# Two graph layers in fp32 on one core: the steps at the seams, the later normalisation and the last group's softmax moved

## The chip, the cores and the metric

The kernel runs on one core of a Trainium2 chip. The time is device microseconds of one execution; three executions were timed, and the median counts. The engines are called as the profile calls them: PE (TensorE, matrix products), PEld (its weight loads), DVE (VectorE), ACT (ScalarE), POOL (GpSimd) and SP (SyncE, which here only issues the DMAs).

## What is computed

The input x is 128 graphs of 64 nodes with 768 features, with one 64x64 adjacency per graph. Everything is fp32. Two layers follow each other:

```python
# layer 0: 12 heads of 64
h = einsum('bnd,ade->bane', x, W);  th = tanh(h)
attn = leaky_relu(th . w_src + (th . w_dst)^T, 0.2)
attn = softmax(where(adj, attn, -999))
feat = elu(attn @ h + b);  gate = sigmoid(x @ H_w.T + H_b)
x = layernorm(x + gate * feat + (1 - gate) * x)
# layer 1: 6 heads of 128
q, k, v = x @ Wq + bq, x @ Wk + bk, x @ Wv + bv
ctx = softmax(q @ k^T / sqrt(128) + where(adj, 0, -9e15)) @ v
x = layernorm(x + ctx @ Wf + bf)
```

## The kernel before

**Tiles and phases.** The 8192 rows (graph, node) are 64 tiles of 128 rows, two graphs each. Phase A computes layer 0 and layer 1's v. It takes the tiles in 32 pairs (NP = 32). Phase B computes the rest of layer 1 in 16 groups of four tiles (NG = 16). Between the phases x1 (the result of layer 0), its transpose and v lie in DRAM (x1_d, xT_d, v_d).

**Products by fewer blocks.** Each large product is taken by block schemes that trade matrix products for additions: in phase A, 7 block products for 8 (class Product, matmuls at L208), in phase B a scheme of 15 steps (R = 15, class Stream, L849). The sums of input blocks are made by `sums` (POOL, L257 to L260) in phase A, by `group_sum` (L819) for q and k and `pair_sum` (L831) for the output projection in phase B. The results of some block products are copied out of PSUM first (`snap`, ACT, L404; the first eviction of a q or k block, ACT, L870), the others are added to them (DVE, L427 and L446; L875 and L892).

**The order of the work** is written out by hand. Each phase has a dictionary of steps; `at(step, f)` appends a call to a step, and `run` makes the calls step after step, in a step in the order in which they were appended. This is the order of each engine's instructions; an engine takes its own in that order, and semaphores hold it where data or a buffer is missing. All DMAs are issued from SP in the same way. A step corresponds to one block product of PE.

**Phase A.** A pair p starts at o = 21p (N = 21). Its seven products with W (h, steps o to o+6) are followed by seven for the gate (G, o+7 to o+13), and seven for v of an earlier pair (V; own V at o+56 for most). Ahead of it come the turns of its input, `xT` (DVE stream transposes, L383, at o-6 and o-5), and `sums` (o-4). Its two tiles go through Tile0, tile 1 with s = o and tile 0 with s = o+5: tanh (L463), multiplications with w_dst and w_src on POOL (L467, L475), the exchange of the destination scores through DRAM (`dst_out`, `exchange`, `dst_in`), `gate_in` (POOL, L580) and `gate` (L584), `add` (POOL L515, leaky ReLU on ACT L518), `mask` and `top` (DVE L522, L526), `exp` (12 ACT instructions, L531), `scale` (DVE L539, POOL L541), `probs` (PE transposes L552), `aggregate` (PE L570), `elu`, `mix1`, `mix2`, `norm1` (DVE, then POOL L295 to L298), `norm2` (ACT, L302), `spill` (store of x1). The last pair has its x1 transposed on PE (`transposed`, L398) instead of being read back. At the start the weights come in: six rows of H_w (`load_hrow`, turned on PE by `hw_blocks`, L358 and L360), W, and the broadcast rows ws_bc, wd_bc, b_bc and hb_bc.

**Phase B.** A group has N = 90 steps: four streams q, k, q, k for the two column halves j, then `scores` and `scores_read`; two output streams F (one for each pair q of the group's tiles) run as fifth and sixth stream beside the next group's work. The softmax of a tile is sm_top (DVE), sm_sub (DVE), sm_exp (ACT, L939), sm_total (DVE), sm_scale (DVE, POOL L948); then `probs` (PE L954, ACT copy L960) and `context` (PE L974). After an output stream norm1 to norm3 normalise its two tiles, norm3 on ACT (L302), and `store` writes them. `load_x` and `add_bf` (POOL, L807) put x1 and the bias into xs ahead of the output stream. The last group's output streams come directly after its own q and k streams, and its tiles end with `end_stats` and `end_norm`.

The steps that the change touches stand in these lines:

```python
at(o - 6, lambda d=d: xT(d, 0))
at(o - 5, lambda d=d: xT(d, 1))
at(o - 4, lambda d=d: sums(d))
for i, s in ((1, o), (0, o + 5)):
    at(s + 19, lambda t=t: t.exp(0))
eng = nc.vector if g <= 1 and k % 2 else nc.gpsimd
sm = o + 4 * R + 8 if last else o + N + 5
t = f + R + 1 + 2 * i
at(t + 3, lambda d=d, q=q, i=i: norm3(d, q, i))
at(t + 5, lambda g=g, d=d, q=q, i=i: store(g, d, q, i))
```

Of the kernel before, what the change touches and what calls it, by code (L numbers as in the profile page):

```python
# [15 lines left out]
P = 128  # L16
# [45 lines left out]
def kernel(  # L62
# [242 lines left out]
    def phase_a(ctx):  # L305
# [35 lines left out]
        ws_bc = rows(k3, w_src.rearrange("a e o -> (a e o)"), "ws_bc")  # L341
        wd_bc = rows(k3, w_dst.rearrange("a e o -> (a e o)"), "wd_bc")
        b_bc = rows(k3, b, "b_bc")
# [18 lines left out]
        for oc in range(NC):  # L362
            load_hrow(oc)
        hb_bc = rows(k3, H_b, "hb_bc")
# [264 lines left out]

        def dense(d, key, i):  # L630
            d[key].matmuls(i)
            d[key].evict(i)
# [17 lines left out]
        for p in range(NP):  # L650
# [11 lines left out]
            if p:  # L662
                at(o - 20, lambda d=d: xb_in(d, 0))
                at(o - 16, lambda d=d: xb_in(d, 1))
                at(o - 6, lambda d=d: xT(d, 0))
                at(o - 5, lambda d=d: xT(d, 1))
            else:
                at(0, lambda d=d: d.update(T=[transposed(t) for t in d["x"]]))
            at(o - 4, lambda d=d: sums(d))
# [5 lines left out]
            for i, s in ((1, o), (0, o + 5)):  # L675
                t = Tile0(p, i)
                at(s + 6 + (i == 0), t.tanh, t.cap)
                at(s + 7, t.dst_mul)
                at(s + 8, t.src_mul)
                at(s + 9, t.dst_sum, t.dst_out, t.exchange)  # L680
                at(s + 10, t.src_sum)
                at(s + 13, t.dst_in)
                at(o + (14 if i else 16), t.gate_in)
                at(o + (16 if i else 18), t.gate)
                at(s + 17, t.add)
                at(s + 18, t.mask, t.top)
                at(s + 19, lambda t=t: t.exp(0))

                at(s + (19 if i else 20), lambda t=t: t.exp(1))
                at(s + 21, lambda t=t: t.scale(0))  # L690
                at(s + 22, lambda t=t: t.scale(1))
                at(s + 24, t.probs)
                at(s + 25, t.aggregate)
                at(s + 26, t.elu)
                at(s + 27, t.mix1)
                at(s + 28, t.mix2)
                at(s + 29, t.norm1)
                at(s + 30, t.norm2)
                at(s + 31, t.spill)
# [13 lines left out]
            else:  # L713
                for i in range(2):
                    at(o + 42 + i, lambda d=d, i=i: x1T(d, i, transposed(d["x"][i])))
# [12 lines left out]
            if p != NP - 4:  # L728
                at(o + (47 if p < NP - 1 else 44), lambda d=d: x1_sums(d))

            v = o + {NP - 4: 84, NP - 2: 50, NP - 1: 45}.get(p, 56)
# [25 lines left out]
        at(o + 30, lambda: load_T4(0))  # L757
        run(events, N * NP + 60)
# [3 lines left out]
    def phase_b(ctx, wq, wk):  # L762
# [167 lines left out]
        def sm_top(d, q, i):  # L930
            d["mx", q, i] = small.tile([P, HEADS], F32, name="mx1")
            nc.vector.tensor_reduce(d["mx", q, i], sm_part(d, q, i), AX.X, ALU.max)
# [103 lines left out]
        for g in range(NG):  # L1036
# [7 lines left out]
            for k in range(len(SUMS)):  # L1044

                eng = nc.vector if g <= 1 and k % 2 else nc.gpsimd
# [13 lines left out]
            for j in range(2):  # L1060
# [7 lines left out]
                for nb in range(3):  # L1068
                    at(b0 + 1 + 2 * nb, lambda d=d, j=j, nb=nb: scores_read(d, j, nb))

            sm = o + 4 * R + 8 if last else o + N + 5
            for q in range(2):
                f = o + ((6 if last else 10) + q) * R
                for i in range(2):
                    t = sm + 4 * (2 * q + i)
# [5 lines left out]
                    at(t + 2, lambda g=g, q=q, i=i: load_v(g, q, i))  # L1081
# [3 lines left out]
                pr = sm + 8 * q + 8  # L1085
# [19 lines left out]
                for i in range(2):  # L1105
# [3 lines left out]
                    at(t + 3, lambda d=d, q=q, i=i: norm3(d, q, i))  # L1109
                    at(t + 5, lambda g=g, d=d, q=q, i=i: store(g, d, q, i))  # L1110
            if g == 0:
                load_adj(0)
# [41 lines left out]
```

## Time and profile before

| | |
|---|---|
| median of 3 runs | 2963.09 us (2961.6 to 2963.64) |
| profiled execution | 2965.06 us |
| its span | 2962.8 us |
| granted PE clock, mean | 0.99 |
| PE busy | 2853.1 us, 18108 instructions |
| DVE busy | 1805.7 us |
| POOL busy | 1649.2 us |
| ACT busy | 1060.1 us |
| DMA, of 16 engines | 33.9% |

The span is the time from the profile's first to its last instruction; the time of the execution holds a little more. A group of the page reads: line, engine, operation, what is written and read (partitions x elements, type), how many; then busy time in all, mean ns of one; then the idle time of the engine just before them and what ended most of it. A row of waits names who waited, for whom, and gives the microseconds in all, how often, and the longest. In the timeline a row begins with start and duration, and the bracket at its end holds the idle time before it and what ended it. A row of windows gives the stretch, its length, and the busy time (instructions) of PE, PEld, DVE, ACT and POOL, then the granted PE clock, the DMA share and GB/s.

### The profile page before, as it was taken

How to read it: one execution, taken by the hardware profiler on the slowest of the kernel's cores; microseconds unless marked ns; L12 is line 12 of the kernel's file. 1: busy time of each engine (PE TensorE's matmuls, PEld its weight loads, DVE VectorE, ACT ScalarE, POOL GpSimd, SP SyncE). 2: the span in 40 equal slices, each digit the busy share in tenths (PEclk: the TensorE clock that was granted, in tenths of full speed). 3: DMA queues.
4: the chain of work that ended last, by engine and by line, in shares of the span. 5: the costliest groups of instructions: out<-in, count | busy, mean ns of one | idle time of the engine just before them, and what ended most of it. 6: DMA issues, size and time to landing. Idle time of an engine off the chain costs nothing.

```text
span 2962.8 us, 50018 instructions
## 1 busy us (share of the span) xinstructions
PE 2853.1 (96%) x18108; PEld 2064.4 (70%) x18108; DVE 1805.7 (61%) x3715; ACT 1060.1 (36%) x2967; POOL 1649.2 (56%) x1712
## 2 busy tenths in 40 slices
PE   7899999999999999999889999999999999999997
PEld 4455555555555555555558888888888888888886
DVE  4667767767667667677565555555555555555556
ACT  3454554554554545545522211222211222221121
POOL 3766566666666665665673454345454345545345
PEclk9999999999999999999999999999999999999999
DMA  6254454453453444544540211212211212221221
GB/s 183 84 148 127 129 148 121 132 149 112 133 149 114 139 136 120 147 125 131 158 161 18 86 59 60 87 55 87 87 66 59 81 56 85 86 70 60 76 81 70
DMA packets 358965, 309.13 MB, mean 104 GB/s; under 512 B 226624, under 2 KB 304192, under 8 KB 358720
## 3 DMA queue, kind: packets, MB, share of 16 engines
q1 hardware_dynamic: 358720, 305.95, 33.6%
q8 instruction: 144, 2.36, 0.3%
q14 instruction: 101, 0.83, 0.1%
HBM read 192.19 MB, written 101.06 MB: 99 GB/s over the span
## 4 chain that ended last, share of the span: by engine, by line
PE 45%; POOL 23%; DVE 15%; ACT 9%; issue 4%; DMA 3%; SPq 1%; POOLq 0%; DVEq 0%
PE X L849 30%; PE X L208 9%; ACT s L531 6%; POOL S L819 5%; POOL gt L580 4%; POOL Sc L831 3%; DVE s L522 2%; DMA xT_d<-T 2%; DVE nmx L526 2%; POOL xs L807 2%; POOL th L475 2%; PE pb L974 2%; POOL s L541 2%; PE pb L914 2%; POOL rstd L295 2%
## 5 line engine op out<-in xcount | busy, mean ns | idle before, releaser
L208 PE MATMUL X<-w,S 128*128 128x384 f32 x2304 | 800.7, 493 | 29.5 <-ACT snap L404 28.0
L849 PE MATMUL X<-S,w 128*128 128x256 f32 x2816 | 668.1, 382 | 20.7 <-ACT q L870 15.9
L208 PEld LDWEIGHTS X<-w,S 128*128 128x128 f32 x2304 | 429.9, 191 | 326.1 <-issue 42.4
L208 PE MATMUL X<-w,T 128*128 128x384 f32 x1728 | 603.6, 492 | 14.7 <-DVE T L383 12.6
L849 PEld LDWEIGHTS X<-S,w 128*128 128x128 f32 x2816 | 522.7, 190 | 99.1 <-issue 21.2
L208 PEld LDWEIGHTS X<-w,T 128*128 128x128 f32 x1728 | 329.7, 193 | 240.3 <-issue 25.1
L831 POOL TENSOR_TENSOR Sc<-cT 128x256 f32<-128x256 f32 x224 | 161.0, 728 | 381.2 <-PE X L849 377.6
L849 PE MATMUL X<-w,Sc 128*128 128x256 f32 x1408 | 328.2, 385 | 3.9 <-DVE xs L892 2.7
L892 DVE TENSOR_TENSOR xs<-xs,X 128x256 f32<-128x256 f32 x512 | 208.6, 419 | 180.0 <-PE X L849 148.7
L849 PEld LDWEIGHTS X<-w,Sc 128*128 128x128 f32 x1408 | 264.9, 191 | 47.0 <-DVE xs L892 9.8
L531 ACT ACTIVATE s<-s,nmx 128x64 f32<-128x64 f32 x768 | 256.1, 335 | 94.6 <-DVE nmx L526 94.6
L875 DVE TENSOR_TENSOR k<-k,X 128x256 f32<-128x256 f32 x320 | 133.5, 421 | 218.6 <-PE X L849 168.4
L875 DVE TENSOR_TENSOR q<-q,X 128x256 f32<-128x256 f32 x320 | 132.0, 419 | 204.7 <-PE X L849 121.0
L541 POOL TENSOR_TENSOR s<-s,rs 128x384 f32<-128x384 f32 x128 | 128.7, 1005 | 214.2 <-DVE rs L539 145.6
L849 PE MATMUL X<-xb,w 128*128 128x256 f32 x960 | 236.6, 379 | 0.0
L302 ACT ACTIVATE xs<-xs,shift,rstd 128x768 f32<-128x768 f32 x62 | 63.7, 1027 | 473.7 <-POOL shift L298 464.7
L404 ACT COPY snap<-X 128x384 f32<-128x384 f32 x288 | 136.0, 473 | 234.2 <-PE X L208 234.2
L467 POOL TENSOR_TENSOR tmp<-th,wd_bc 128x768 f32<-128x768 f32 x64 | 138.2, 2160 | 133.7 <-ACT th L463 133.7
L870 ACT ACTIVATE k<-X,bk_c 128x256 f32<-128x256 f32 x192 | 90.9, 474 | 305.2 <-PE X L849 305.2
L849 PEld LDWEIGHTS X<-xb,w 128*128 128x128 f32 x960 | 181.2, 190 | 24.0
L948 POOL TENSOR_TENSOR s<-s,rs 128x384 f32<-128x384 f32 x64 | 53.0, 828 | 242.1 <-DVE rs L947 219.3
L870 ACT ACTIVATE q<-X,bq_c 128x256 f32<-128x256 f32 x192 | 88.8, 470 | 258.6 <-PE X L849 258.6
(106 smaller groups left out, 4102.6 us busy)
## 6 DMA issues: line engine op xcount, KB each, us to landing
xb<-in_x_dram SPq DMA_DIRECT2D x64, 384.0 KB
s<-dst_d SPq DMA_DIRECT2D x128, 192.0 KB
x_d<-xb SPq DMA_DIRECT2D x64, 384.0 KB
xT_d<-T SPq DMA_DIRECT2D x64, 384.0 KB
v_d<-v SPq DMA_DIRECT2D x128, 192.0 KB
xb<-xT_d SPq DMA_DIRECT2D x32, 768.0 KB
xb<-v_d SPq DMA_DIRECT2D x256, 96.0 KB
xs<-x_d SPq DMA_DIRECT2D x64, 384.0 KB
```

What stands on the lines that cost most here:

```text
L208: nc.tensor.matmul(o, self.lhsT(i, c), rhs, start=first and c == 0, stop=last and c == CH - 1, skip_group_check=True,)
L404: nc.scalar.copy(t, ps)
L467: nc.gpsimd.tensor_tensor(self.tmp, self.th, wd_bc, ALU.mult)
L531: nc.scalar.activation(self.s[:, a], self.s[:, a], AF.Exp, bias=self.nmx[:, a : a + 1], accum_out=self.sm[:, a : a + 1],)
L541: nc.gpsimd.tensor_tensor(t, t, rs[:, :, None].to_broadcast([P, A // 2, S]), ALU.mult)
L580: nc.gpsimd.tensor_tensor(self.g, self.g, hb_bc, ALU.add)
L819: eng.tensor_tensor(t, group_part(d, r0), group_part(d, r1), op)
L831: nc.gpsimd.tensor_tensor(t, pair_part(d, q, r0), pair_part(d, q, r1), op)
L849: nc.tensor.matmul(ps, self.lhsT(r, slot, c), self.rhs(r, slot, c), start=start and c == 0, stop=stop and c == 1, skip_group_check=True,)
L870: nc.scalar.activation(o[:, b], ps, AF.Identity, bias=bias[:, hd : hd + 1], scale=1.0 if positive else -1.0)
L875: nc.vector.tensor_tensor(o[:, b], o[:, b], ps, ALU.add if positive else ALU.subtract)
L892: nc.vector.tensor_tensor(o, o, ps, ALU.add if positive else ALU.subtract)
```

## The change

Six things are changed; no product, sum or DMA of phase A is added or removed.

- The loads of the broadcast rows wd_bc, ws_bc and b_bc are issued after the six H_w rows instead of before.
- `xT` and `sums` of pairs 1, 2 and 31 come 7, 5 and 4 steps earlier (`lead`).
- In pairs 0 and 1, everything of a tile from `exp` to `spill` comes two steps later (`slow`), and tile 1's exps are appended at the very end of their step (`late`).
- In the last pair tile 0 has s = o+3, its x1T transposes come at o+41 and o+40 with tile 1 first, its x1 sums at o+42, its V at o+43.
- In phase B norm3 comes at t+4+2i and the store at t+6+2i. In group 0 the q and k sums whose number divided by 3 leaves 2 are made by POOL and the others by DVE, and `load_adj(0)`, with the fill that it makes, comes at step 16.
- The last group's softmax starts two steps earlier. Its maximum is negated, and `sm_top_exp` makes six exps with the maximum as bias and the sum as a second output; `sm_sub` and `sm_total` are left out there. `probs` comes at t+7 and `context` at t+10, the second pair of tiles 13 steps after the first. The second half's `scores_read` come in successive steps.

```diff
@@ -338,9 +338,6 @@
             )
-        ws_bc = rows(k3, w_src.rearrange("a e o -> (a e o)"), "ws_bc")
-        wd_bc = rows(k3, w_dst.rearrange("a e o -> (a e o)"), "wd_bc")
-        b_bc = rows(k3, b, "b_bc")
         w1 = weight_tile(1)
@@ -361,6 +358,9 @@
             load_hrow(oc)
+        wd_bc = rows(k3, w_dst.rearrange("a e o -> (a e o)"), "wd_bc")
+        ws_bc = rows(k3, w_src.rearrange("a e o -> (a e o)"), "ws_bc")
+        b_bc = rows(k3, b, "b_bc")
         hb_bc = rows(k3, H_b, "hb_bc")
@@ -627,6 +627,8 @@
+        late = {}
         def dense(d, key, i):
@@ -662,17 +664,23 @@
                 at(o - 16, lambda d=d: xb_in(d, 1))
-                at(o - 6, lambda d=d: xT(d, 0))
-                at(o - 5, lambda d=d: xT(d, 1))
+                lead = {1: 7, 2: 5, NP - 1: 4}.get(p, 0)
+                at(o - 6 - lead, lambda d=d: xT(d, 0))
+                at(o - 5 - lead, lambda d=d: xT(d, 1))
+                at(o - 4 - lead, lambda d=d: sums(d))
             else:
                 at(0, lambda d=d: d.update(T=[transposed(t) for t in d["x"]]))
-            at(o - 4, lambda d=d: sums(d))
+                at(0, lambda d=d: sums(d))
             at(o, lambda d=d: start_h(d))
...
                 at(o + 7 + i, lambda d=d, i=i: dense(d, "G", i))
-            for i, s in ((1, o), (0, o + 5)):
...
+            slow = 2 if p < 2 else 0
+            for i, s in ((1, o), (0, o + (5 if p < NP - 1 else 3))):
                 t = Tile0(p, i)
@@ -684,19 +692,23 @@
                 at(s + 18, t.mask, t.top)
-                at(s + 19, lambda t=t: t.exp(0))
-
-                at(s + (19 if i else 20), lambda t=t: t.exp(1))
-                at(s + 21, lambda t=t: t.scale(0))
-                at(s + 22, lambda t=t: t.scale(1))
-                at(s + 24, t.probs)
-                at(s + 25, t.aggregate)
-                at(s + 26, t.elu)
-                at(s + 27, t.mix1)
-                at(s + 28, t.mix2)
-                at(s + 29, t.norm1)
-                at(s + 30, t.norm2)
-                at(s + 31, t.spill)
+                z = s + slow
+                if slow and i:
+                    late.setdefault(z + 19, []).extend((lambda t=t: t.exp(0), lambda t=t: t.exp(1)))
+                else:
+                    at(z + 19, lambda t=t: t.exp(0))
+                    at(z + (19 if i else 20), lambda t=t: t.exp(1))
+                at(z + 21, lambda t=t: t.scale(0))
+                at(z + 22, lambda t=t: t.scale(1))
+                at(z + 24, t.probs)
+                at(z + 25, t.aggregate)
+                at(z + 26, t.elu)
+                at(z + 27, t.mix1)
+                at(z + 28, t.mix2)
+                at(z + 29, t.norm1)
+                at(z + 30, t.norm2)
+                at(z + 31, t.spill)
@@ -712,7 +724,7 @@
                 for i in range(2):
-                    at(o + 42 + i, lambda d=d, i=i: x1T(d, i, transposed(d["x"][i])))
+                    at(o + 41 - i, lambda d=d, i=i: x1T(d, i, transposed(d["x"][i])))
@@ -726,9 +738,9 @@
             if p != NP - 4:
-                at(o + (47 if p < NP - 1 else 44), lambda d=d: x1_sums(d))
-
-            v = o + {NP - 4: 84, NP - 2: 50, NP - 1: 45}.get(p, 56)
+                at(o + (47 if p < NP - 1 else 42), lambda d=d: x1_sums(d))
+            v = o + {NP - 4: 84, NP - 2: 50, NP - 1: 43}.get(p, 56)
             if p == NP - 4:
@@ -755,6 +767,8 @@
         at(o + 30, lambda: load_T4(0))
+        for step, fs in late.items():
+            events.setdefault(step, []).extend(fs)
         run(events, N * NP + 60)
@@ -927,9 +941,18 @@
-        def sm_top(d, q, i):
+        def sm_top(d, q, i, negate=False):
             d["mx", q, i] = small.tile([P, HEADS], F32, name="mx1")
-            nc.vector.tensor_reduce(d["mx", q, i], sm_part(d, q, i), AX.X, ALU.max)
+            nc.vector.tensor_reduce(d["mx", q, i], sm_part(d, q, i), AX.X, ALU.max, negate=negate)
+        def sm_top_exp(d, q, i):
+            s, mx, sm = sm_part(d, q, i), d["mx", q, i], small.tile([P, HEADS], F32, name="sm1")
+            for h in range(HEADS):
+                nc.scalar.activation(
+                    s[:, h], s[:, h], AF.Exp, bias=mx[:, h : h + 1], accum_out=sm[:, h : h + 1]
+                )
+            d["sm", q, i] = sm
@@ -1043,7 +1066,7 @@
-                eng = nc.vector if g <= 1 and k % 2 else nc.gpsimd
+                eng = nc.vector if (k % 3 != 2 if g == 0 else g == 1 and k % 2) else nc.gpsimd
                 if g == 0:
@@ -1066,23 +1089,31 @@
                 for nb in range(3):
-                    at(b0 + 1 + 2 * nb, lambda d=d, j=j, nb=nb: scores_read(d, j, nb))
-
-            sm = o + 4 * R + 8 if last else o + N + 5
+                    at(b0 + 1 + (1 if last and j else 2) * nb, lambda d=d, j=j, nb=nb: scores_read(d, j, nb))
+            sm = o + 4 * R + 6 if last else o + N + 5
             for q in range(2):
                 for i in range(2):
-                    t = sm + 4 * (2 * q + i)
+                    t = sm + 4 * i + (13 if last else 8) * q
+                    at(t + 2, lambda g=g, q=q, i=i: load_v(g, q, i))
+                    if last:
+                        at(t, lambda d=d, q=q, i=i: sm_top(d, q, i, True))
+                        at(t + 2, lambda d=d, q=q, i=i: sm_top_exp(d, q, i))
+                        at(t + 5, lambda d=d, q=q, i=i: sm_scale(d, q, i))
+                        at(t + 7, lambda d=d, q=q, i=i: probs(d, q, i))
+                        at(t + 10, lambda d=d, q=q, i=i: context(d, q, i))
+                        continue
                     at(t, lambda d=d, q=q, i=i: sm_top(d, q, i))
...
                     at(t + 7, lambda d=d, q=q, i=i: sm_scale(d, q, i))
-                    at(t + 2, lambda g=g, q=q, i=i: load_v(g, q, i))
                     at(t + 10, lambda d=d, q=q, i=i: probs(d, q, i))
...
-                pr = sm + 8 * q + 8
+                pr = sm + (5 + 13 * q if last else 8 + 8 * q)
                 for k in range(len(SUMS)):
@@ -1106,10 +1137,11 @@
                     at(t + 1, lambda d=d, q=q, i=i: norm2(d, q, i))
-                    at(t + 3, lambda d=d, q=q, i=i: norm3(d, q, i))
-                    at(t + 5, lambda g=g, d=d, q=q, i=i: store(g, d, q, i))
+                    at(t + 4 + 2 * i, lambda d=d, q=q, i=i: norm3(d, q, i))
+                    at(t + 6 + 2 * i, lambda g=g, d=d, q=q, i=i: store(g, d, q, i))
             if g == 0:
-                load_adj(0)
+                at(16, lambda: load_adj(0))
                 bf_bc = rows(k1, bf, "bf_bc")
```

## Prediction

> **What bounds the kernel.** I read the page's busy shares first, then TensorE's busy time stage by stage, its waits in each stage, and last the timeline around the waits that the change touches.
>
> ```profile
> PE 2853.1 (96%) x18108; PEld 2064.4 (70%) x18108; DVE 1805.7 (61%) x3715; ACT 1060.1 (36%) x2967; POOL 1649.2 (56%) x1712
> L849 PE MATMUL X<-S,w 128*128 128x256 f32 x2816 | 668.1, 382 | 20.7 <-ACT q L870 15.9
> ```
>
> TensorE sets the time; 2962.8 - 2853.1 = 109.7 us of the span is all that better order can win. The change adds no matmul and removes none, so only this idle time, and matmuls slowed after a wait, can move. By stage (window length, then PE, PE weight load, DVE, ACT, POOL busy):
>
> ```profile
> 0.00:175.00 175.00, 139.58 (x667) 84.08 (x668) 99.68 (x165) 75.20 (x232) 99.13 (x91) 0.93 0.50 141
> 1397.00:1540.00 143.00, 119.11 (x552) 71.99 (x553) 92.51 (x136) 57.39 (x166) 92.62 (x80) 0.93 0.49 153
> 1713.00:2850.00 1137.00, 1122.19 (x8403) 963.86 (x8404) 605.57 (x1612) 238.85 (x464) 551.66 (x677) 1.00 0.22 74
> 2850.00:2963.00 113.00, 97.47 (x779) 82.13 (x777) 62.65 (x169) 16.49 (x28) 55.48 (x76) 0.94 0.19 63
> ```
>
> Idle: 35.4 at the start, 23.9 at the seam between the phases, 14.8 in thirteen steady groups of phase B, 15.5 at the end (8.1 of it after the last matmul). The change leaves the other 20 us alone. TensorE's waits in the steady groups are a single row, and at the seams mixed ones (start, seam, end, a row or two of each):
>
> ```profile
> PE X L849 <- ACT q L870: 14.8, 13, 1.2
> ...
> PE X L208 <- ACT snap L404: 14.4, 4, 6.6
> PE X L208 <- DVE T L383: 7.0, 2, 5.6
> PE pa L358 <- DMA gt<-in_L_gnn_H_w_dram: 3.7, 1, 3.7
> ...
> PE X L208 <- DVE T L383: 5.6, 1, 5.6
> PE X L208 <- ACT snap L404: 5.0, 3, 4.0
> ...
> PE pb L954 <- POOL s L948: 3.3, 1, 3.3
> ```
>
> The steady one in the timeline:
>
> ```profile
> 1771.44 2.06 ACT L302 ACTIVATE xs<-xs,shift,rstd 128x768 f32<-128x768 f32 x2 [2.38 <-POOL shift L298]
> 1773.41 0.45 ACT L870 ACTIVATE q<-X,bq_c 128x256 f32<-128x256 f32 x1
> 1774.01 2.18 PE L849 MATMUL X<-S,w 128*128 128x256 f32 x9 [1.14 <-ACT q L870]
> ```
>
> Two normalisations of 1.03 us stand on ScalarE ahead of the q eviction that TensorE waits for.
>
> **What the Trainium skill says.** "PSUM — Partial Sum Buffer", Engine vs sequencer instructions: the queues of ScalarE, VectorE and GpSimdE are strict FIFO. The trace agrees: the q eviction above sat behind both normalisations. "TensorE: Matmul & The Clock Gate", Part 1, What's actually happening: after an idle window of about 3.4 us the clock halves until some 3.4 us of work. The trace agrees: after the 6.57 us wait at 63.93 six matmuls took 4.18 us, elsewhere 2.10. "ScalarE: Activation LUTs", Rules: about 0.3 us an ACTIVATE plus 0.83 ns an element; the trace has 0.335 us for 64 elements. "GPSIMD Engine Reference", §3: an add is 1.96 times as long as on VectorE; the trace has 1.27 us for 128x512 at L819, and the S0 share below rests on it.
>
> **Part 1, later normalisation in phase B.** norm3 goes from step t+3 to t+4 for tile 0 and t+6 for tile 1. On ScalarE the order beside each second output stream was q(step 4), norm3(0), norm3(1), q(7), exp, q(11); it becomes q(4), norm3(0), q(7), exp, norm3(1), q(11), in 14 places. norm3(0) still starts at 1771.44, when its shift is there, and ends at 1772.47. The data of q(7) came at about 1772.38, so q(7) ends at about 1772.93 instead of 1773.86, and TensorE, ready at 1772.87, resumes about 1772.98: 0.1 of the 1.14 us stays. Saved 14 x 1.03 = **14.4 us**. Behind norm3(1) stand q(11), wanted from about 1774.7, while norm3(1) ends about 1774.3 after the exp (0.51), and tile 1's store. That store goes about a microsecond later on SP's queue, in the same order there; behind it stand load_v, and load_x at 1785.64 whose data POOL first uses at 1798.87, so it is covered; uncovered, it would cost that microsecond. Bounds: 12 (0.2 us left each time) to 15.9 (all of the page's row).
>
> **Part 2, the start.** The three broadcast loads go behind the six H_w rows, two of 384 KB each to a wait: the 3.7 us gt wait goes, but the w0 sums on DVE (11th of 0.57 us operations from 16.3, so about 22.6) catch TensorE after 2.2. Pairs 1 and 2 get their turns and sums 7 and 5 steps earlier: the same 4 turns (2.45 us on DVE) and 4 POOL adds (0.99 + 1.69 + 0.99 + 0.99 = 4.66), but now in front of the previous pair's multiplies, gate and score add (L515). Tile 1's 12 exps (12 x 0.335 = 4.0 us) go behind the next pair's first snap. Pair 1: L515 starts about 56.7 instead of 54.98, then 1.47 + Prelu 0.84 + gate 0.83, so the snap ends about 60.4 against 63.78, and pair 1's W products end about 3.8 earlier. Pair 2: the 5.64 us turn wait goes, but sums stand ahead of L515 and tile 0 of pair 0 is itself two steps later; I put the snap's start about 108.3 instead of 111.69. That holds the gain at 3.4 to 3.8 in all, half speed after the snap wait staying. **-3.5**; bounds -9 (POOL's idle 2.54 and 3.71 us near 90 to 95 takes the sums in, and all three snaps come early) to +2 (none of it does, with later probs).
>
> **Part 3, the last pair.** The timeline before:
>
> ```profile
> 1407.87 0.55 POOL L295 TENSOR_TENSOR rstd<-rstd,neg_half 128x1 f32<-128x1 f32 x1 [3.71 <-DVE rstd L294]
> 1410.66 3.59 POOL L580 TENSOR_TENSOR gt<-gt,hb_bc 128x768 f32<-128x768 f32 x2
> 1414.22 1.46 POOL L515 TENSOR_TENSOR s<-s,src 128x768 f32<-128x768 f32 x1
> 1423.16 2.26 PE L208 MATMUL X<-w,S 128*128 128x384 f32 x5 [4.03 <-ACT snap L404]
> ```
>
> Pair 31's turns move ahead of pair 30's mix and batch norm on DVE (rstd +2.1), its sums (4.66) ahead of that gate and add: L515 starts at about 1422, not 1414.22. Here the exps (pair 30 isn't slow) still stand before the first snap, so W2 starts about 1429.5: late by 6.4, half speed included about 7, though the 5.63 us turn wait is gone. Given back: tile 0 two steps earlier takes the probs waits (0.92 + 2.89, and half speed, about 2.1); the x1 transposes, tile 1 first, and x1 sums and V two steps earlier take most of the 4.4 us wait. By V's last product I have +0.3. Group 0's sums on two engines (S0 0.7 on DVE against 1.3) and fill moved to step 16 take 1.1 from the q wait of 2.5. **-0.8**; bounds -8 (delay absorbed, waits gone) to +6 (delay not given back).
>
> **Part 4, the last group.** Out: four subtractions and four totals on DVE (8 x 0.55). In: 6 exps a tile with sum (6 x 0.335 = 2.0 us against 0.51) on ScalarE, busy 16.5 of 113 us. But probs come at step 73, not 78. Their scale on POOL stands behind add_bf (3.57) and the context sums, free at about 2904:
>
> ```profile
> 2899.62 3.57 POOL L807 TENSOR_TENSOR xs<-xs,bf_bc 128x768 f32<-128x768 f32 x2
> 2906.40 0.90 PE L954 MATMUL pb<-ident,s 128*128 128x128 f32 x3 [3.33 <-POOL s L948]
> ```
>
> TensorE arrives about 2898: a wait of 6.7 for 3.3 (+3.4), with slow matmuls 1.0 more; later the Sc wait (1.2), xs wait (2.3) and its half speed (1.9) go, as POOL has caught up. **-1**; bounds -6 to +3. The tail after the last matmul keeps its chain.
>
> Sum: -14.4 - 3.5 - 0.8 - 1.0 = -19.7. The profiled execution took 2965.06 (span 2962.8): 2945.4. The median is 2.0 below it: **2943**.
>
> **Rivals.** A, the seams do what the edits look like: 9 at the start, 8 at the last pair, 6 at the end, and 14.4: 2963 - 37 = 2926. For it: the named waits are there, and each edit lies before one. Against: POOL is 57 to 65% busy in these windows and the moved sums pass its queue. B, only the normalisation pays, seams cost: +6 - 14.4 = 2955; for it, the 6.4 us above. C, slower: GpSimd's queue becomes the bound at the seams, no idle absorbing what is put ahead. Price 4.66 for pair 1, 4.66 for pair 2, 9.1 for pair 31 with half speed, 6.2 at the end: 24.6 against 14.4, so 2973. It decides once more than 59% of that price isn't regained. Against: POOL's idle stretches before rstd (3.71). D, no change: norm3(1) delays q(11) as much as it did q(7), the wait only moves: 2963 - 14 + 14 = 2963 less what the seams give. Against: exp and norm3 fit before q(11) with 0.4 us to spare, which is thin.
>
> **From cases to numbers.** The forecast (2935 to 2951) 0.56, A 0.22, B 0.08, C 0.09, D 0.05. A measurement of this kernel can tell 0.2%, 5.9 us, from no change. Forecast, A and B are faster: 0.86; D same 0.05; C slower 0.09. The range leaves out C, D and the far end of A (0.06): 2926 to 2956.
>
> **What would show it.** Right: q waits in steady groups of about 0.1 us, the group from 88.3 to about 87.3; no gt wait over 1.5; the snaps of pairs 1 and 2 about 3.4 earlier; pair 31's W2 some 6 later than now against pair 30's last G, regained by its last V; a probs wait of 6 to 7 on POOL at the end. Wrong: a wait on q after step 11; longer snap waits; a last-group gap past 7 us. The least certain step is the 6.4 us of pair 31, worked by hand from queue order, and next the POOL wait at the end.

## Result and the profile after

The changed kernel takes 2965.14 us (median of four runs, 2964.37 to 2968.44), the kernel before beside it 2963.36. The ratio is 1.0007, with a 95% interval of 0.999 to 1.0025: no difference that can be told from zero. The forecast was 2943, with a range of 2926 to 2956.

The profiled span of the changed kernel is 2963.0 us, of the kernel before 2962.8. From its page, the busy times and the group of TensorE with the most idle time in front of it:

```profile
PE 2847.2 (96%) x18108; PEld 2063.0 (70%) x18108; DVE 1812.2 (61%) x3710; ACT 1063.3 (36%) x3011; POOL 1642.1 (55%) x1709
...
L208 PE MATMUL X<-w,S 128*128 128x384 f32 x2304 | 804.1, 495 | 61.5 <-ACT snap L404 55.9
```

The group stood at 29.5 us of idle time before; it is 61.5, nearly all for the snap on ScalarE. The rows of waits of TensorE at the start, at the seam between the phases (two rows) and in the last group:

```profile
PE X L208 <- ACT snap L404: 28.2, 5, 17.0
...
PE X L208 <- ACT snap L404: 22.3, 2, 18.2
PE pa L570 <- ACT pt L557: 7.3, 1, 7.3
...
PE pb L977 <- POOL s L971: 6.8, 2, 6.1
```

The snap waits were 14.4 and 5.0 us in these stretches. The wait for the probs copy (L557) is new. In the steady groups of phase B no wait of TensorE is left at all. The same stretches by busy time (length, then PE, PE weight load, DVE, ACT, POOL, granted clock, DMA share, GB/s):

```profile
0.00:175.00 175.00, 131.09 (x639) 78.17 (x640) 101.54 (x154) 69.89 (x220) 96.28 (x88) 0.90 0.50 139
...
1397.00:1540.00 143.00, 111.73 (x579) 66.90 (x578) 90.38 (x135) 55.26 (x162) 86.42 (x78) 0.90 0.43 131
...
1713.00:2850.00 1137.00, 1135.86 (x8642) 976.66 (x8635) 613.65 (x1630) 240.24 (x470) 561.78 (x690) 1.00 0.22 74
...
2850.00:2963.00 113.00, 96.19 (x778) 81.33 (x776) 58.32 (x161) 22.99 (x72) 54.78 (x76) 0.95 0.19 62
```

In the third row TensorE is busy 1135.9 of 1137 us, where it was 1122.2. In the first it has 131.1 of 175, where it had 139.6.

Busy times of fixed windows don't give a ledger, since the work slides through them. Marks do: the start of the same instruction in both traces. I took evictions on ScalarE: the last copy of an h block (L425), the copy of a gate block (L425) and the k evictions of phase B.

| mark | before | changed | difference |
|---|---|---|---|
| pair 0, last h copy | 36.58 | 33.41 | -3.2 |
| pair 3, last h copy | 172.06 | 180.29 | +8.2 |
| pair 30, gate copy | 1406.85 | 1414.82 | +8.0 |
| group 0, first k eviction | 1545.01 | 1560.00 | +15.0 |
| group 15, last k eviction | 2881.73 | 2881.55 | -0.2 |
| end of the span | 2962.8 | 2963.0 | +0.2 |

So the parts, as differences of neighbouring rows, forecast beside measured: start -3.5, measured +8.0 (to pair 30's gate copy); last pair and group 0's sums -0.8, measured +7.0; phase B -14.4, measured -15.2; last group -1.0, measured +0.4. The sum is +0.2 where -19.7 was forecast. Phase B did what was expected; two seams cost what it gained. The -3.2 in the first row is largely scatter of the first loads, as the experiments show. The profiled execution of the kernel before was 2.0 us above its median, and the medians differ by 1.8 us where the two spans differ by 0.2.

The phase B gain in the timeline, ScalarE beside a second output stream:

```profile
1785.41 1.03 ACT L302 ACTIVATE xs<-xs,shift,rstd 128x768 f32<-128x768 f32 x1 [2.38 <-POOL shift L298]
1786.34 0.45 ACT L884 ACTIVATE q<-X,bq_c 128x256 f32<-128x256 f32 x1
1786.70 0.51 ACT L962 ACTIVATE s<-s 128x384 f32<-128x384 f32 x1
1787.11 1.01 ACT L302 ACTIVATE xs<-xs,shift,rstd 128x768 f32<-128x768 f32 x1
1788.94 0.47 ACT L884 ACTIVATE q<-X,bq_c 128x256 f32<-128x256 f32 x1 [0.82 <-PE X L863]
```

The normalisation of tile 0 ends and the q eviction follows at once, as worked out; the second normalisation stands behind the exp and is done 0.8 us before the next q eviction can start, which then waits for TensorE and not the reverse.

The start, around pair 2's first snap, in the kernel before:

```profile
89.55 1.81 POOL L467 TENSOR_TENSOR tmp<-th,wd_bc 128x768 f32<-128x768 f32 x1 [2.54 <-ACT th L463]
...
96.12 1.80 POOL L475 TENSOR_TENSOR th<-th,ws_bc 128x768 f32<-128x768 f32 x1
...
103.34 1.46 POOL L515 TENSOR_TENSOR s<-s,src 128x768 f32<-128x768 f32 x1
...
111.69 0.45 ACT L404 COPY snap<-X 128x384 f32<-128x384 f32 x1
...
112.29 4.18 PE L208 MATMUL X<-w,S 128*128 128x384 f32 x6 [6.61 <-ACT snap L404]
```

And in the changed kernel:

```profile
92.88 1.85 POOL L467 TENSOR_TENSOR tmp<-th,wd_bc 128x768 f32<-128x768 f32 x1 [4.42 <-ACT th L463]
94.69 1.71 POOL L257 TENSOR_TENSOR S<-T 128x384 f32<-128x384 f32 x1
98.03 1.71 POOL L259 TENSOR_TENSOR S<-T 128x384 f32<-128x384 f32 x1
100.65 1.79 POOL L475 TENSOR_TENSOR th<-th,ws_bc 128x768 f32<-128x768 f32 x1
...
108.87 1.47 POOL L515 TENSOR_TENSOR s<-s,src 128x768 f32<-128x768 f32 x1
...
106.24 1.03 ACT L302 ACTIVATE xb<-xb,shift,rstd 128x768 f32<-128x768 f32 x1 [13.07 <-POOL shift L298]
111.86 0.46 ACT L404 COPY snap<-X 128x384 f32<-128x384 f32 x1
...
112.46 3.97 PE L208 MATMUL X<-w,S 128*128 128x384 f32 x6 [17.04 <-ACT snap L404]
```

TensorE has done pair 2's first two products and stands for 17.04 us. The wait for the turns (5.64 before) is gone, and the wait for the snap, 6.61 before, has taken it in and grown. The snap itself comes no earlier than before (111.86 beside 111.69), though pair 0's copy came 3.2 us earlier. On the way back from the snap: score add (L515) at 108.87 instead of 103.34, the multiply L475 at 100.65 instead of 96.12, and between L467 and L475 the four sums, of which three took 1.59 to 1.71 us where the same form takes 0.99 alone.

Pair 31 shows the same order:

```profile
1417.68 0.55 POOL L295 TENSOR_TENSOR rstd<-rstd,neg_half 128x1 f32<-128x1 f32 x1 [5.55 <-DVE rstd L294]
1420.48 0.99 POOL L257 TENSOR_TENSOR S<-T 128x384 f32<-128x384 f32 x1
1424.40 3.56 POOL L580 TENSOR_TENSOR gt<-gt,hb_bc 128x768 f32<-128x768 f32 x2
1427.91 1.47 POOL L515 TENSOR_TENSOR s<-s,src 128x768 f32<-128x768 f32 x1
...
1436.27 0.45 ACT L404 COPY snap<-X 128x384 f32<-128x384 f32 x1
...
1436.86 3.54 PE L208 MATMUL X<-w,S 128*128 128x384 f32 x5 [18.21 <-ACT snap L404]
```

And the new wait in the seam, at tile 0 of pair 31 (DVE, ACT, PE):

```profile
1506.30 1.90 DVE L612 SCALAR_TENSOR_TENSOR xb<-xb,pt 128x768 f32<-128x768 f32 x1
...
1508.29 0.86 ACT L557 COPY pt<-pa 128x384 f32<-128x384 f32 x2 [6.40 <-DVE xb L612]
...
1508.82 0.37 PE L570 MATMUL pa<-h,pt 64*64 64x64 f32 x1 [7.29 <-ACT pt L557]
```

The copy of tile 0's transposed probabilities waits for the last mix instruction of tile 1, since the two use one buffer of 128 x 768, and tile 0 now runs two steps earlier. Last, the probs of the last group:

```profile
2898.92 3.56 POOL L821 TENSOR_TENSOR xs<-xs,bf_bc 128x768 f32<-128x768 f32 x2
2903.12 0.83 POOL L971 TENSOR_TENSOR s<-s,rs 128x384 f32<-128x384 f32 x1
...
2904.00 0.90 PE L977 MATMUL pb<-ident,s 128*128 128x128 f32 x3 [6.06 <-POOL s L971]
```

A wait of 6.06 us on the scale that stands behind add_bf on POOL; the forecast had 6.7.

### The profile page after: what moved, and what is told of

The parts are those of the page before. It is cut to its first block, busy times and chain, and to the rows that moved or that the text cites. A ratio compares the mean times of both kernels' runs of the same rounds, so it can differ in the third digit from the quotient of the medians.

```text
span 2963.0 us, 50040 instructions
## 1 busy us (share of the span) xinstructions
PE 2847.2 (96%) x18108; PEld 2063.0 (70%) x18108; DVE 1812.2 (61%) x3710; ACT 1063.3 (36%) x3011; POOL 1642.1 (55%) x1709
## 4 chain that ended last, share of the span: by engine, by line
PE 60%; DVE 14%; POOL 10%; ACT 8%; DMA 5%; issue 3%; SPq 1%; POOLq 0%; DVEq 0%; ACTq 0%
PE X L863 42%; PE X L208 12%; ACT s L531 5%; POOL gt L580 3%; DMA xT_d<-T 2%; DVE s L522 2%; PE pb L997 2%; PE pb L928 2%; POOL s L541 2%; DVE nmx L526 1%; POOL th L475 1%; DVE pt L611 1%; DMA s<-dst_d 1%; DVE pt L602 1%; DVE pt L603 1%
## 5 line engine op out<-in xcount | busy, mean ns | idle before, releaser
L208 PE MATMUL X<-w,S 128*128 128x384 f32 x2304 | 804.1, 495 | 61.5 <-ACT snap L404 55.9
L889 DVE TENSOR_TENSOR q<-q,X 128x256 f32<-128x256 f32 x320 | 132.2, 420 | 188.6 <-PE X L863 131.1
L467 POOL TENSOR_TENSOR tmp<-th,wd_bc 128x768 f32<-128x768 f32 x64 | 136.9, 2139 | 131.5 <-ACT th L463 131.5
L833 POOL TENSOR_TENSOR S<-xb 128x512 f32<-128x512 f32 x103 | 130.7, 1282 | 84.1 <-DMA xb<-xT_d 57.2
```

The costliest lines, as they stand in the source:

```text
L208: nc.tensor.matmul(o, self.lhsT(i, c), rhs, start=first and c == 0, stop=last and c == CH - 1, skip_group_check=True,)
L467: nc.gpsimd.tensor_tensor(self.tmp, self.th, wd_bc, ALU.mult)
L833: eng.tensor_tensor(t, group_part(d, r0), group_part(d, r1), op)
L889: nc.vector.tensor_tensor(o[:, b], o[:, b], ps, ALU.add if positive else ALU.subtract)
```

## Experiments

Theory 1 was that phase B's part pays in full and that two seams give it back. For the start the question was whether the delay of pairs 0 and 1 (theory S) or the early turns and sums (rival L) cost. Where a result below has no ratio, the kernel was timed in one execution alone, so differences of two or three microseconds between such totals decide nothing. All trace comparisons below are by marks: "to pair 3" is the time from pair 0's last h copy to pair 3's, which leaves the first loads out (135.5 before; 146.9 changed); "to h" and "to k" go from pair 30's gate copy to pair 31's last h copy and to group 0's first k eviction (29.7 and 138.2 before; 35.5 and 145.2 changed). Profiles of the same code scatter. Seven kernels that are the same up to pair 3 gave 144.8 to 146.9 there. Seven with pair 31 and group 0 as changed gave 145.0 to 148.4 to k, with a mean of 146.8; the changed kernel's 145.2 is near the low end, and what a single profile tells at k is not better than about 3 us. The cause of the first scatter stands in the traces. TensorE waits 3.0 us for a snap in pair 0's V, between pair 2's gate and pair 3's h; after it come, in the changed kernel and in the run with pair 31's early turns and sums alone:

```profile
157.92 4.21 PE L208 MATMUL X<-w,T 128*128 128x384 f32 x6 [3.00 <-ACT snap L404]
161.92 3.08 PE L208 MATMUL X<-w,S 128*128 128x384 f32 x6
...
157.46 2.20 PE L208 MATMUL X<-w,T 128*128 128x384 f32 x6 [3.01 <-ACT snap L404]
159.50 2.10 PE L208 MATMUL X<-w,S 128*128 128x384 f32 x6
```

After the same wait the same twelve matmuls run slowly in one execution and at full speed in another. So matmuls can be slow after a wait that is shorter than the 3.4 us in the prediction; what decides whether they are was not tried.

**Later normalisation alone.** On the kernel before:

```diff
-                    at(t + 3, lambda d=d, q=q, i=i: norm3(d, q, i))
-                    at(t + 5, lambda g=g, d=d, q=q, i=i: store(g, d, q, i))
+                    at(t + 4 + 2 * i, lambda d=d, q=q, i=i: norm3(d, q, i))
+                    at(t + 6 + 2 * i, lambda g=g, d=d, q=q, i=i: store(g, d, q, i))
```

> The kernel before with only the later normalisation of phase B. Theory 1 (this part pays in full and the seams gave it back): no wait on the q eviction in the steady groups, and 14 to 15.5 us less than the kernel before, so about 2948.5. Rival (the later normalisation only moves the work to another wait, and the changed kernel's phase B gains for another reason): within 4 us of the kernel before.

Measured: 2947.56 us against 2962.29, ratio 0.9949 (0.9933 to 0.9966). Theory 1 holds and its rival falls. TensorE's waits in the steady groups come to 0.2 us. This kernel is faster than the kernel before and the changed kernel.

**The changed kernel without the delay.**

```diff
-            slow = 2 if p < 2 else 0
+            slow = 0
```

> The changed kernel with the delay of two steps in pairs 0 and 1, and the exps moved behind the snap, taken back; the earlier turns and sums stay. Measured at the copy of pair 3's last h block on ScalarE (172.06 before, 180.29 changed). Theory S (the delay puts the previous pair's norm chain in front of the snap on ScalarE): the 17 us snap wait goes and the copy comes at 169 to 174, the total 6 us or more below the changed kernel. Rival L (the earlier sums on POOL do it): copy at 178 or later, total within 3 us of the changed kernel.

Measured: 2962.81 us; the h copy of pair 3 at 173.90, 141.1 to pair 3. TensorE's wait for the snap at the start:

```profile
PE X L208 <- ACT snap L404: 30.9, 4, 17.4
```

A mixed answer. The copy came early enough for S, but the long wait that S blamed on the delay is still there, 17.4 us, and the total is only 2.3 us lower. So the long wait belongs to the early work, and the delay costs some 4 to 6 us elsewhere (144.8 to 146.9 to pair 3 with it, 141.1 without).

**The changed kernel without the early turns and sums of pairs 1 and 2.**

```diff
-                lead = {1: 7, 2: 5, NP - 1: 4}.get(p, 0)
+                lead = {NP - 1: 4}.get(p, 0)
```

> The changed kernel with turns and sums of pairs 1 and 2 at their old steps; the delay stays. Theory S: the copy of pair 3's last h block still comes at 176 or later, with a snap wait of 8 us or more in pair 2. Rival L: copy at 168 to 173, no snap wait over 7 us.

Measured: 2957.56 us; copy at 172.58, 139.2 to pair 3.

```profile
PE X L208 <- DVE T L383: 11.8, 2, 10.4
PE X L208 <- ACT snap L404: 8.0, 4, 3.5
```

By its letter this is rival L: the copy lies in its range and no snap wait is over 3.5 us. But to pair 3 it is still 4.8 us later than with neither part (134.4, in the next experiment), which is the delay's, and the long wait is now one for the turns, 10.4 us. Neither theory had that. Along the pairs the delay first wins: pair 1's last h copy came 36.7 after pair 0's (41.7 before), because the snap no longer stands behind 12 exps. Then it loses all of that and more: pair 2's turns stand on VectorE behind a mix that is two steps later.

**Of the start only the load order.** `slow = 0` and `lead` for pair 31 alone.

> The changed kernel with neither the delay nor the earlier turns of pairs 1 and 2; of the start only the order of the loads is changed. All theories: the gt wait at 0.6, and the copy of pair 3's last h block at about 172.06 - 3.2 = 168.9; the total 11 us below the changed kernel, about 2954. If the gain of the loads is lost again in pair 1, the copy comes at 171 or later.

Measured: 2958.80 us; 134.4 to pair 3; copy at 169.42. The seam loss of the start is gone, as all theories had it; the total is 6.3 us lower and not 11, since this profile took 148.2 to k and had a late first copy. The gain of the loads isn't there: pair 0's last h copy came at 35.01. Over all profiles of this study it came at 33.2 to 36.6 with the old order of the loads (four profiles, mean 34.3) and at 32.5 to 35.0 with the new (fourteen, mean 33.4). The wait for the first H_w rows (tile gt), 3.7 us in the profile before, was 1.8, 2.2 and 4.3 us in the three others with the old order. With the new order it was 0.6 us in the changed kernel's profile, but 2.3 to 2.4 in nine of the fourteen: on the whole it is shorter, not gone.

**Early work in pair 1, not in pair 2, no delay.**

```diff
-                lead = {1: 7, 2: 5, NP - 1: 4}.get(p, 0)
+                lead = {1: 7, NP - 1: 4}.get(p, 0)
...
-            slow = 2 if p < 2 else 0
+            slow = 0
```

> The changed kernel with the earlier turns and sums in pair 1 (and 31) but not in pair 2, and without the delay. Measured from pair 0's last h copy on ScalarE to pair 1's (41.7 before, 44.7 with both leads and no delay) and pair 3's (135.5 before, 141.1 with both leads and no delay, 134.4 with neither). Theory A (each early set of sums costs by itself, by standing ahead of the score add on POOL): 44.7 to pair 1 and 136.5 to 138.5 to pair 3. Rival (pair 2's loss follows from pair 1's): 140 or more to pair 3, or back to 135.5 if pair 1's loss is regained.

Measured: 2959.11 us; 45.1 to pair 1 and 138.5 to pair 3. Theory A holds: each early set costs by itself, pair 1's 4.1 us (138.5 against 134.4), pair 2's 2.6 more (141.1), which is little above the scatter.

**Early work as changed, the delay in pair 0 alone.**

```diff
-            slow = 2 if p < 2 else 0
+            slow = 2 if p < 1 else 0
```

> The changed kernel with the delay in pair 0 alone; leads as changed. Measured as above to pair 3's last h copy (146.9 changed). Theory A (pair 1's delay puts its norm chain ahead of pair 3's start and costs the 5 to 6 us lost there): 139 to 143, and no 3 us snap wait in pair 0's V. Rival (the loss in pair 3 follows from the lateness of POOL in pair 2): 145 or more.

Measured: 2965.72 us; 144.1 to pair 3, between the two expectations. Pair 1's delay did cost what pair 3 lost: from pair 2's gate to pair 3's h the time is 29.9 again (33.2 to 35.0 with the delay). But without it pair 2's snap is back behind the exps and waits 23.3 us, so the time to pair 3 is only 0.7 to 2.8 us shorter than with both delays, and the total is no shorter. The parts of the start are not additive one by one, and none of them pays with the leads in place.

The start as a table, to pair 3 in us:

| | no delay | delay in pair 0 | delay in pairs 0 and 1 |
|---|---|---|---|
| no early work | 134.4 | 134.1 (below) | 139.2 |
| early in pair 1 | 138.5 | | |
| early in pairs 1 and 2 | 141.1 | 144.1 | 144.8 to 146.9 |

Each row below the first is later than the first: by 4.1 and 6.7 without the delay, by 10.0 with the delay in pair 0, and by 5.6 to 7.7 with it in both. Except for the last field these are single profiles.

**The last pair as before**, in the changed kernel: `lead` without pair 31, s = o+5 for tile 0, x1T, x1 sums and V at their old steps.

> The changed kernel with pair 31 as before: neither earlier turns and sums nor tile 0, x1 transposes and V two steps earlier. Measured from pair 30's last gate copy on ScalarE to pair 31's last h copy (29.7 before, 35.5 changed) and to the first k eviction of group 0 (138.2 before, 145.2 changed). All theories: 29.7, and 137 to 138.5, since group 0's sums on two engines and the later fill stay; total about 7 us below the changed kernel. If group 0's part costs, the second stays above 140.

Measured: 2958.66 us; 30.8 to h, 138.3 to k. The seam's loss is gone. From V's last addition to the first k eviction it took 20.3 us (21.2 before): group 0's sums on two engines bring 0.9 us here, about as forecast (1.1). Over all profiles it is less: with the new sums this stretch took 20.3 us in nine and 21.9 to 22.0 in five, where in the two traces compared (changed kernel, load order alone) the same wait of 2.4 us is followed by slow matmuls in the one and not in the other. With the old sums it took 21.2 in all four. The mean gain is 0.3 us.

**Pair 31's early turns and sums alone**: as that kernel, with `lead` of 4 for pair 31.

> The changed kernel with only the earlier turns and sums of pair 31; its tile 0, x1 transposes and V are at their old steps. Theory P (the sums cost 5.8 at the h copy, and the 7.3 us wait for the one probs buffer comes from tile 0's two steps): 35.5 to the h copy, no wait over 4 us for the probs copy, and 139 to 142 to the first k eviction. Rival (the buffer wait comes from the lateness that the sums make): that wait stays at 5 or more and the k eviction at 144 or later.

Measured: 2960.69 us; 36.0 to h, 142.9 to k; no wait for the probs copy. Theory P holds in its first part: the early work costs 5.2 to 6.3 us at the h copy and still 4.6 at k (142.9, against an expected 139 to 142).

**Pair 31's tile 0, x1 and V alone**: `lead` without pair 31, the rest as changed.

> The changed kernel with pair 31's turns and sums at their old steps; tile 0, x1 transposes and V stay two steps earlier. Theory P: 29.7 to the h copy, the wait for the probs copy still 5 us or more, 140 to 144 to the first k eviction. Rival (the wait comes from the sums' lateness): no such wait over 3 us, 138 or less.

Measured: 2957.07 us; 29.7 to h, 139.2 to k, wait for the probs copy 7.3 us. That wait comes from tile 0's two steps, as P said, but it cost 1 us at k, less than the expected 140 to 144 (1.9 us if one counts from pair 31's h copy, which came 1.1 us earlier here than in the run with the last pair as before).

**A buffer of its own for tile 0's probabilities**, in the changed kernel:

```diff
-                self.pt = k3.tile([P, D], F32, name="pt").rearrange("p (j n) -> p j n", n=P)
+                self.pt = k3.tile([P, D], F32, name="tmp" if self.p == NP - 1 and not self.i else "pt").rearrange("p (j n) -> p j n", n=P)
```

> The changed kernel, but pair 31's tile 0 puts its transposed probabilities in the buffer of the w_dst product, which nothing uses any more at that point, instead of the one probs buffer that tile 1's mix still reads. Theory P: the 7.3 us wait for the probs copy falls under 2 us and the first k eviction comes at 138 to 142 after pair 30's last gate copy (145.2 changed). Rival (the matmuls would have waited for the late scale on POOL anyway): a wait of 4 us or more on POOL in its place, 144 or later.

Measured: 2966.74 us; 36.5 to h, 147.6 to k. TensorE's waits at the seam:

```profile
PE X L208 <- ACT snap L404: 23.1, 3, 18.2
PE X L208 <- POOL S L258: 2.5, 1, 2.5
PE pa L570 <- ACT tmp L557: 0.8, 1, 0.8
```

The buffer wait fell from 7.3 to 0.8, and nothing was won: 2.5 us for the sums of x1 and 1.5 for rstd on POOL came in its place, as the rival had it, and 147.6 lies among the 145.0 to 148.4 of the seven profiles with the shared buffer. A wait that was long in the trace was not one that set the end.

**The same without the early sums of pair 31.** The last edit with `lead` without pair 31.

> The changed kernel with pair 31's turns and sums at their old steps, tile 0, x1 transposes and V two steps earlier, and tile 0's probabilities in their own buffer. Measured from pair 30's last gate copy to V's last addition (116.9 before, 118.8 with the shared buffer, 124.9 changed, 125.6 changed with own buffer). Theory P (the buffer wait is what keeps tile 0's two steps from paying): 113 to 116. Rival (behind the buffer the x1 chain of the same tiles sets the start of V's second half, whatever the buffer): 117.5 to 120.

Measured: 2957.44 us; V's last addition 118.3 after pair 30's gate copy (118.8 with the shared buffer), k at 140.3. The rival holds here too: behind the buffer the x1 chain sets V's start (a 3.2 us wait for rstd on POOL). Which instruction of it is the first to be late was not tried.

**The last group as before**, in the changed kernel: its old softmax, steps and `scores_read`.

> The changed kernel with the last group's softmax of the kernel before. Measured from the last k eviction to the end of the span (81.1 before, 81.5 changed). Theory: the earlier probs only move the POOL wait, so this gives 80.7 to 81.5 and a total within 2 us of the changed kernel. Rival (the shorter softmax pays 2 us or more behind another loss): 83 or more.

Measured: 2963.68 us; 81.3 from the last k eviction to the end (81.5 changed, 81.1 before). As the theory had it, the end is neutral in this pair of profiles: the probs wait is 3.3 us again, and the Sc and xs waits (1.3 and 2.7) are back. Over all profiles the new end took 81.2 to 82.3 us (eleven, mean 81.6) and the old one 80.0 to 81.5 (seven, mean 80.6). So it gains nothing and may cost about 1 us.

**Turns early, sums at their old step**, on the kernel with the later normalisation alone, since the early work had two halves:

```diff
+                lead = {1: 7, 2: 5, NP - 1: 4}.get(p, 0)
-                at(o - 6, lambda d=d: xT(d, 0))
-                at(o - 5, lambda d=d: xT(d, 1))
+                at(o - 6 - lead, lambda d=d: xT(d, 0))
+                at(o - 5 - lead, lambda d=d: xT(d, 1))
```

> The kernel with only the later normalisation of phase B, and with the turns of pairs 1, 2 and 31 earlier by 7, 5 and 4 steps while their sums stay at the old step. Measured from pair 0's last h copy to pair 3's (135.4 without, 141.1 with turns and sums early) and from pair 30's last gate copy to pair 31's last h copy (29.7 without, 35.5 to 36.5 with both). Theory A (the sums ahead of the score add on POOL cost): 132 to 136 and 27.5 to 30, total 2945 to 2948, since the turn wait goes but the snap behind the exps does not come earlier. Rival D (the turns on VectorE, ahead of mix and rstd, cost): 138 or more and 33 or more, total 2953 or more.

Measured: 2950.97 us, ratio 0.9964 (0.995 to 0.9978), 3.4 and 5.3 us over the two measurements of the later normalisation alone (2947.56, and 2945.72 below); 136.8 to pair 3 and 32.7 to h. Between the two theories, and in pair 31 both halves cost. In pair 31's timeline (POOL, then PE):

```profile
1407.59 0.55 POOL L295 TENSOR_TENSOR rstd<-rstd,neg_half 128x1 f32<-128x1 f32 x1 [5.55 <-DVE rstd L294]
1413.92 1.47 POOL L515 TENSOR_TENSOR s<-s,src 128x768 f32<-128x768 f32 x1
...
1422.86 2.90 PE L208 MATMUL X<-w,S 128*128 128x384 f32 x4 [14.30 <-ACT snap L404]
```

From the gate copy (1404.73) the score add comes at 9.2 us; it was 7.4 before and is 13.1 in the changed kernel. So of the 5.7 us by which the score add is late, the turns on VectorE, ahead of rstd, make 1.8 and the sums on POOL 3.9. And the turn wait is gone here, yet the snap wait is 14.30 us: TensorE gets to the snap sooner and waits longer for it.

**Two tries at a better seam.** First the later normalisation, the new load order, group 0's sums, and the delay with the exps behind the snap in pair 0 alone (`slow = 2 if p < 1 else 0`, no early work, pair 31 and the end as before):

> What the runs so far speak for: later normalisation in phase B, the changed order of the loads, group 0's sums on two engines, and the delay with exps behind the snap in pair 0 alone; no leads, pair 31 and the end as before. If pair 1's 5 us gain (seen where the delay stood without leads) lasts: 130 to 132 to pair 3's last h copy, total about 2943. If pair 2 loses it again by a late turn, as where both pairs were delayed: 134 to 136, total 2946 to 2948, no better than the later normalisation alone (2947.6).

Measured: 2945.52 us, ratio 0.9943 (0.9926 to 0.9959); 134.1 to pair 3. Pair 1 won its 5 us (36.7) and pair 2 lost 3.6 of them by a turn wait of 10.4, as the second expectation had it. Then the same with the delay also in pair 30 (`slow = 2 if p in (0, NP - 2) else 0`), beside the later normalisation alone:

> Later normalisation in phase B, changed load order, group 0's sums on two engines, and the delay with exps behind the snap in pairs 0 and 30; no early turns or sums, pair 31 and the end as before. From pair 30's last gate copy to pair 31's last h copy (29.7 before) and to V's last addition (116.9 before). Theory X (the snap behind the exps sets pair 31's start): 24 to 27, and 113 to 116 if it lasts, total about 2942 to 2944. Rival (the delayed mix makes the turn as late as the snap was): 28.5 to 31, total 2945 or more.

Measured: 2948.45 us, ratio 0.9954 (0.9939 to 0.9969); 26.0 to h, so the snap behind the exps does set pair 31's start, but 120.3 to V's last addition (116.9 before): lost again. What takes it stays open. The total is the rival's.

> The later normalisation of phase B alone, as in the first run, for comparison on the same chip: 2947 to 2948; 29.7 and 116.9 in pair 31.

Measured: 2945.72 us, ratio 0.9945 (0.9928 to 0.9961); 30.4 and 117.4 in pair 31. No variant is faster than the one edit of phase B by more than the intervals.

## Why the prediction was wrong

**Part 1 was right.** 14.4 us forecast; 15.2 by marks (14.3 in the kernel with it alone), 14.7 and 15.3 as medians of that kernel. A steady group went from 88.3 to 87.3 us, as forecast. The queue argument held to the tenth: the q eviction starts as the first normalisation ends. Rival D (the wait only moves) is refuted here, although it named the total that came.

**Part 2 failed at three steps**: a gain too many, a chain too short, and a cost left out. The load order: "the 3.7 us gt wait goes" took one profile's wait as the kernel's, and with the new order most profiles still show 2.3 us of it. The means of 33.4 and 34.3 leave some 0.9 us of the forecast 2.2, and the scatter is larger than that. The sign of the whole part was decided at "I put the snap's start about 108.3": it was 111.86. The chain there was right in its members and too short. L467 came at 92.88, not 89.55, behind a tanh that waits on ScalarE for the delayed elu, and that elu in turn stood behind pair 2's early turns on VectorE. The sums took 6.0 us between L467 and L475, not 4.66, since VectorE's mix ran beside them and both were slower (its 0.96 us form took 1.63 and more). "GPSIMD Engine Reference", §1 Specifications, of the Trainium skill has the two engines share their SBUF interfaces, with contention for VectorE instructions with two SBUF inputs, which the mix instructions are; this trace agrees. Another 1.0 us came between L475 and the score add, where the delayed tile's rstd steps now stand. And the sum had no term for what pair 1's delay does to pair 3: 3 to 5 us, as the run with the delay in pair 0 alone shows. "That holds the gain at 3.4 to 3.8" stopped the walk one pair too soon. From pair 0's copy to pair 3's the part cost 11.4 us in the changed kernel's profile and 9.4 in four others with the same code. Pair 1 gained 0.4 us from copy to copy (41.3 for 41.7), pairs 2 and 3 lost 5.6 and 6.2.

**Part 3: the lateness was right, "given back" was not.** The 6.4 us for pair 31's W2 was measured as 5.7 (22.0 us from gate copy to W2 against 16.3), with the rstd and the score add where the order put them. The step that failed is "By V's last product I have +0.3"; V's last addition came 8.0 us late (124.9 for 116.9). The figure doesn't follow from its own terms either: 7 less 0.92, 2.89, 2.1 and most of 4.4 is below -1. It assumed that the later waits (0.92, 2.89, 4.4) are slack that a late pair uses up. By themselves the early turns and sums leave 4.6 us at the k eviction, and tile 0's two steps add 1 us instead of taking 2. Together they make 7.0 in the changed kernel's profile and 8.5 in the mean of seven, over the mean of three before. The 7.3 us buffer wait, which I had not seen although both names are in the code, is real, but removing it won nothing. Why the two together cost more than their sum of 5.6 stays open; the difference is within the scatter.

**Part 4 was right in its wait and a little off in its sum**: 6.06 for 6.7, then +0.4 instead of -1 (+1.0 in the means of all profiles); about the size of the scatter.

**The rivals.** Rival C had the greater part of the mechanism: what is put ahead in GpSimd's queue at the seams is not taken in by idle time, and little of it is regained. In pair 31 that is 3.9 of the 5.7 us; the other 1.8 are the turns on VectorE. It priced pairs 1, 2 and 31 at 18.4 us, and the marks have 18.4 there (11.4 from pair 0's copy, 7.0 at the last pair). That the figures are equal is luck: a part of the loss is the delay's and not the sums', and other profiles of the same code have 9.4 at the start and up to 10.2 at the last pair. Its 6.2 us at the end did not come. I gave it 0.09, since I weighed it as one case against the sum of small gains. The named waits were what made the seams look like gains: at pairs 1, 2 and 31 a turn wait (1.4, 5.6, 5.6) stood in front of a snap wait (6.6, 6.6, 4.0) on the same path, and the later one ends last.

## What to carry to other kernels

When a product waits first for one thing and soon after for another, moving the first one earlier only lengthens the second: find the wait that ends last, here score add, leaky ReLU, exps and snap, and ask what the move puts ahead of it on each in-order queue. A delay of one tile's chain by two steps has to be followed through until the last pair that meets its later members, on all engines. And a wait read from one profile at the start of a kernel, where loads set it, should be compared over several profiles before it is entered as a gain.

## What was not expected of the hardware

A wait of 7.29 us could be taken off TensorE without any gain, since other waits took its place. The same instructions up to pair 3 took 144.8 to 144.9 us in four profiles, 145.4 in one and 146.8 to 146.9 in two: after the same wait of 3.0 us twelve matmuls took 4.0 us in the four, 5.7 in the one and 6.9 in the two. POOL's 128 x 384 add took 0.99 us alone and 1.59 to 1.71 beside VectorE's mix.
